# Cross attention, eight batches on one core: the maximum of half 1 is taken off by accumulating DMAs, and three left sums are made later

## The chip, the cores and the metric

The kernel runs on one core of one Trainium2 chip. A core has five engines with an instruction queue each: PE (TensorE, the matmuls, with its weight loads shown apart as PEld), DVE (VectorE), ACT (ScalarE), POOL (GpSimd) and SP (SyncE, which here only issues DMAs). Sixteen DMA engines move data for all queues. The time is device microseconds of one launch; the median of three runs of the kernel before is 704.6 us (703.48 to 705.7).

## The reference

For each of 8 batches there are two inputs of 512 channels by 1024 positions, `x1` and `x2`. Cut to what matters:

```python
q = einsum('bcn,dc->bnd', x1, Wq) + bq            # d = 64
k = einsum('bcn,dc->bdn', x2, Wk) + bk[:, None]
v = einsum('bcn,dc->bdn', x2, Wv) + bv[:, None]   # 512 channels
attn = softmax(einsum('bnd,bdm->bnm', q, k), axis=2)
out = einsum('bcm,bnm->bcn', v, attn) + x1
```

All of it is float32. The softmax runs over the 1024 keys m, for each of the 1024 queries n.

## The kernel before, in words

**The mathematics.** The scores are kept transposed, keys on the partitions and queries along the free axis. The kernel first makes y = x2 times exp(scores), divides its columns by the sums of the exponentials, and then makes Wv times y, adds the bias and x1. Both large products ("first" with `stage` y, "second" with `stage` o) are done with seven block products in place of eight (`MULT`): each factor is cut into two by two blocks, and DVE makes sums and differences of blocks (S1 to S4 on the left, T1 to T4 on the right). Three of the seven block products of the first product, numbers 2, 3 and 4, are cut once more in the same manner (`multiply_2`, `multiply_3`, `multiply_4`, with `inner_left` and `inner_right` for their sums and L351 for their matmuls).

**The tiles.** `e[h]` holds the exponentials of half h of the queries (h = 0 for queries 0 to 511, 1 for the rest): 128 partitions x 2 halves of the keys x 4 key tiles x 512 queries. Block 11 of the right factor is `e[0][:, 0]`, 21 is `e[0][:, 1]`, 12 is `e[1][:, 0]` and 22 is `e[1][:, 1]`. The blocks of x2, transposed, are `a["11"]` to `a["22"]`. S1 = 21 + 22, S2 = S1 - 11, S3 = 11 - 21 (written over block 21), S4 = 12 - S2. `u1`, `u5`, `u6`, `r` are tags of scratch tiles; a tag with one buffer makes the next user wait until the last reader of the tile is done.

**A period.** `period` handles one batch s. PE runs in this order: first(1), `multiply_2`, first(6), the scores of half 0 of the next batch n, the queries of the batch after it (L148, `ps_q`), first(5), first(7), `multiply_3`, the scores of half 1 of n, the keys of the batch after it (`ps_k`), `multiply_4`, and then the seven second products 1, 6, 2, 5, 7, 3, 4. In periods 1 to 7 this is all; in period 0 the products are not cut a second time. Period 6 has no queries and keys to project, and period 7 has no next batch.

**The softmax of the next batch** lies inside the period of this one. ACT copies the scores of a half from PSUM into `e[h]` (L197, L199). `fold` (L211) takes the maximum over the key tiles on DVE, `highest` folds the two key halves (L215) and lets POOL reduce over the partitions with one PARTITION_ALL_REDUCE into `top[h]` (L220), which has the same value on all partitions. `exponentials` then takes `top` off each key tile on DVE (L248, 128 x 1024 elements) and lets ACT raise it to the exponential (L249), four times for a half.

**The sums of the exponentials.** For half 0, `start_sum` copies the first key tile on ACT (L507) and adds the other three with accumulating DMAs that POOL issues, each waiting for the one before (L509). `total` folds the two key halves on DVE (L215), lets POOL reduce over the partitions (L225) and sends one row on by a small DMA (`few`, L227). For half 1 the sum is made on DVE (`sums`). `shares` makes the reciprocals (L233) and spreads them with two DMAs (L235, L237) over `den`.

**What sets the order.** The schedule is written by hand: each engine executes its instructions in the order of the source, and the framework puts in the waits. A wait stops all that stands behind it on that engine's queue. DMAs with accumulation are issued by POOL, plain ones by SP (and the copies of q by ACT).

**The places that the change touches**, in the order of the period:

- after first(5): the exponentials of half 0 of n (L248, L249), `start_sum`, `inner_right(s, 3, ...)`, and then the left sums S1, S2, S3 of n (L109), three DVE instructions of 128 x 1024 elements;
- after the scores of half 1: the folds of the maximum of half 1, `highest`, and for s.b > 0 `total(n, 0)`;
- `multiply_4`: its inner products are copied by ACT (L360) into `d` and `v`; `complete` (L422) adds v to d on DVE, two more additions (L432) bring it into `u6`. The tile `v` has the tag `u1`, which is also the tag of the tile that second(1) is copied into (L312);
- `evict_y(s, "21")` (L462, L464) makes the last block of y, which second(2) reads;
- the second products: ACT copies the banks of 1, 6 and 5 (L312) into u1, u6, u5 for later additions; the chain 1, 6, 5, 3 runs on one pair of PSUM banks, so product 6 may add to a bank only after ACT has copied product 1 out of it;
- the four exponentials of half 1 of n stand after second(6) and after second(5);
- `evict_o` adds bank, bias and an earlier copy on DVE (L496), or, for block 12, copies the bank with the bias on ACT (L492, into tag `r`); then POOL issues a DMA that adds x1 to it (L499), and SP writes it out (L500).

In period 0 the order differs a little: there S1, S2 and S3 of batch 1 and the inner sums of its `multiply_2` stand between the last blocks of the result, and `total(1, 0)` behind second(2).

Of the kernel before, what the change touches and what calls it, by code (L numbers as in the profile page):

```python
# [10 lines left out]
AF = mybir.ActivationFunctionType  # L11
ALU = mybir.AluOpType
# [3 lines left out]
def kernel(  # L16
# [46 lines left out]
    nc = tc.nc  # L63
    P = 128
# [3 lines left out]
    H = 512  # L68
    MH = N // P // 2
# [64 lines left out]
    def sum_a(s, *ks):  # L134
        for k in ks:
            if k != "S3":
                s.a[k] = sb.tile([P, MH, C // 2], F32, tag=f"a{k}", name=f"a{k}_{s.b}")
        left_sums(s.a, *ks)
# [74 lines left out]
    def fold_halves(s, h, op):  # L213
        f = s.mx[h]
        nc.vector.tensor_tensor(f[:, 0, :], f[:, 0, :], f[:, 1, :], op)  # L215
# [6 lines left out]
    def total(s, h):  # L222
        fold_halves(s, h, ALU.add)
        s.den[h] = sb.tile([P, H], F32, tag="den", name=f"den_{s.b}_{h}", bufs=2)
        nc.gpsimd.partition_all_reduce(s.den[h], s.mx[h][:, 0, :], P, ReduceOp.add)  # L225
        s.few[h] = sb.tile([P, H // P], F32, tag="few", name=f"few_{s.b}_{h}", bufs=2)
        nc.gpsimd.dma_start(  # L227
            s.few[h], s.den[h][0:1, :].rearrange("o (p f) -> o p f", p=P)
        )
# [9 lines left out]
    def first_exponentials(s, g, i):  # L239
# [2 lines left out]
        nc.vector.tensor_tensor(e, e, s.top[0], ALU.subtract)  # L242
        nc.scalar.activation(e, e, AF.Exp)  # L243

    def exponentials(s, h, i):
        e = s.e[h][:, :, i, :]
        top = s.top[h].unsqueeze(1).to_broadcast([P, 2, H])
        nc.vector.tensor_tensor(e, e, top, ALU.subtract)  # L248
        nc.scalar.activation(e, e, AF.Exp)  # L249
# [77 lines left out]
    def inner_left(s, i, x, tag):  # L327

        v = {f"{p + 1}{q + 1}": x[:, ts(q, MH // 2), ts(p, P)] for p in range(2) for q in range(2)}
        sums = sb.tile([P, 4, MH // 2, P], F32, tag=tag, name=f"aI{i}_{s.b}")  # L330
        for z, (k, x, y, op) in enumerate(LEFT):
            v[k] = sums[:, z]
            nc.vector.tensor_tensor(v[k], v[x], v[y], op)
        s.inner[i] = v

    def inner_right(s, i, x, tag):

        v = {
            f"{q + 1}{r + 1}": x[:, ts(q, MH // 2), ts(r, H // 2)] for q in range(2) for r in range(2)
        }  # L340
        sums = sb.tile([P, 4, MH // 2, H // 2], F32, tag=tag, name=f"eI{i}_{s.b}")
        for z, (k, x, y, op) in enumerate(RIGHT):
            v[k] = sums[:, z]
            nc.vector.tensor_tensor(v[k], v[x], v[y], op)
        s.inner[i, "t"] = v
# [18 lines left out]
    def inner_bank(s, i, z):  # L364
        return ps_s.tile([P, 2, H], F32, tag="sc", name=f"ps_i{i}{z}_{s.b}")[:, 0, left]
# [35 lines left out]
    def multiply_onto(s, i, d_tag, v_tag):  # L401

        b0, b1 = (s.bank[MULT[i][2], j] for j in range(2))
        chain, third = inner_bank(s, i, 0), inner_bank(s, i, 2)
        d = sb.tile([P, 2, 2, H // 2], F32, tag=d_tag, name=f"d{i}_{s.b}")
        v = sb.tile([P, 2, H], F32, tag=v_tag, name=f"v{i}_{s.b}")[:, 0, left]
        for z, ps, opens, *copies in (
            (1, chain, True, d[:, 0, 0, :]),  # L410
            (7, third, True, v),
            (6, chain, False, d[:, 1, 0, :]),
            (2, b0[:, left], False),
            (5, chain, False, d[:, 0, 1, :], d[:, 1, 1, :]),
            (4, b1[:, left], False),
            (3, b0[:, right], False),
        ):
            inner_product(s, i, z, ps, opens, *copies)

        def complete():  # L420
            both = v.unsqueeze(1).to_broadcast([P, 2, H // 2])
            nc.vector.tensor_tensor(d[:, 1], d[:, 1], both, ALU.add)  # L422

        return d.rearrange("p j a n -> p j (a n)"), complete

    def multiply_4(s):

        d, complete = multiply_onto(s, 4, "u5", "u1")
        complete()
        for j in range(2):  # L430
            u6 = s.tmp[6][:, j, :]
            nc.vector.tensor_tensor(u6, u6, d[:, j, :], ALU.add)  # L432
# [175 lines left out]
    def period(s, n, nn, nnn):  # L608

        def first(i):
            multiply(s, "y", i, s.a, s.t, MH)

        def second(i):
            multiply(s, "o", i, w, s.y, 2)

        open_t(s)
        if n is None:
            load_x(s, x1)  # L620
        first(1)
        if s.b == 0:
            head_second(s, n)
        sum_e(s, "T1", "T2")
        if s.b == 0:
            total(s, 0)
        else:
            shares(s, 0)
        if n:
            load_a(n, "11")  # L630
        if s.b == 0:
            first(2)
            evict_y(s, "11", (1,))
            keys(n)
            load_x(nn, x1)
            sum_t4(s)
            sums(s, 1)
            shares(s, 0)
        else:
            evict = multiply_2(s)  # L640
            if s.b > 1:
                sums(s, 1)
            evict()
            sum_t4(s)
            sum_a(s, "S4")
            if s.b == 1:
                sums(s, 1)
        sum_e(s, "T3")
        if n:
            load_a(n, "21", "22")  # L650
        first(6)
        if s.b:
            inner_right(s, 4, s.t["T4"], "eT2")
            inner_left(s, 3, s.a["S4"], "aI3")

        def next_queries():
            queries(nn)
            load_x(nn, x2)

        def next_keys():  # L660
            keys(nn)
            if nnn:
                load_x(nnn, x1)

        if n:
            scores_and(n, 0, "c", next_queries if nn else nothing)
            for i in range(1, MH):
                fold(n, 0, i, "max", ALU.max)
            highest(n, 0)
        shares(s, 1)  # L670
        first(5)
        if n:
            for i in range(MH):
                exponentials(n, 0, i)
            start_sum(n, 0)
        if s.b:
            inner_right(s, 3, s.t["22"], "eT1")
            if n:
                sum_a(n, "S1", "S2", "S3")
        first(7)  # L680
        if s.b > 1:
            inner_left(s, 4, s.a["22"], "a12")
        if s.b:
            evict_y(s, "22", (1,))
            multiply_3(s)()
            for k in ("11", "12", "22"):
                evict_y(s, k, (2,))
        else:
            evict_y(s, "11", (2,))
            evict_y(s, "22")  # L690
            first(3)
            evict_y(s, "12", (1,))
        if s.b == 1:
            inner_left(s, 4, s.a["22"], "a12")
        if n:
            scores_and(n, 1, "a", next_keys if nn else nothing)
        sum_y(s, "T1")
        sum_y(s, "T2")
        if n:
            if s.b == 0:  # L700
                left_sums(w, "S1", "S2", "S3", "S4")
            for i in range(1, MH):
                fold(n, 1, i, "max", ALU.max)
            highest(n, 1)
            if s.b:
                total(n, 0)
        if s.b:
            multiply_4(s)
        else:
            first(4)  # L710
        if n:
            load_a(n, "12")
        evict_y(s, "21")
        second(1)
        sum_y(s, "T3")
        sum_y(s, "T4")
        second(6)
        if n:
            exponentials(n, 1, 0)
            exponentials(n, 1, 1)  # L720
        second(2)
        evict_o(s, "11")
        if s.b == 0:
            total(n, 0)
        second(5)
        if n:
            exponentials(n, 1, 2)
            exponentials(n, 1, 3)
        second(7)
        evict_o(s, "22")  # L730
        if n:
            if s.b:
                inner_left(n, 2, n.a["12"], "aS4")
            else:
                sum_a(n, "S1")
            second(3)
            evict_o(s, "12")
            if s.b:
                inner_right(n, 2, n.e[0][:, 1], "eT4")
            else:  # L740
                sum_a(n, "S2")
            second(4)
            evict_o(s, "21")
            if s.b == 0:
                sum_a(n, "S3")
                inner_left(n, 2, n.a["12"], "aS4")
                inner_right(n, 2, n.e[0][:, 1], "eT4")
        else:
            second(4)
            evict_o(s, "21")  # L750
            second(3)
            evict_o(s, "12")
# [37 lines left out]
```

## Time and profile before

| | us |
|---|---|
| median of 3 runs | 704.6 (703.48 to 705.7) |
| the profiled execution, its own time | 704.53 |
| its span in the profile | 702.8 |
| PE busy | 689.1, 2144 matmuls |
| DVE busy | 601.5, 730 instructions |
| ACT busy | 251.4, 390 instructions |
| POOL busy | 173.6, 135 instructions |
| POOL-issued DMAs (queue q0) | 29.96 MB, 25.2% of 16 engines' span |
| SP-issued DMAs (queue q1) | 70.26 MB, 29.3% of 16 engines' span |

The span is what the profiler saw from the first to the last instruction; 1.7 us of the execution's own time lie outside it. PE ran at full clock throughout (0.999 of it granted). A busy PE means that matmuls follow one another; how far each could be shorter is not in this number. The chain of waits, which follows the work that ended last back to its start, lies on PE for 80% of the span and on DVE for 12%.

The groups that the change removes, moves or adds to:

| line and group | count | mean of one | what it is |
|---|---|---|---|
| L248 DVE subtract, 128 x 1024 | 60 | 1251 ns | maximum taken off; 28 of them are half 1 of batches 1 to 7 |
| L249 ACT exponential, 128 x 1024 | 60 | 1054 ns | |
| L109 DVE S1, S2, S3, 128 x 1024 | 8 each | 1219, 1315, 1218 ns | |
| L220 POOL reduction of the maximum | 16 | 2026 ns | |
| L225 POOL reduction of the sum | 16 | 3497 ns | |
| L509 POOL issue of an accumulating DMA | 21 | 1205 ns | |
| L312 ACT copy of a bank, 128 x 512 | 48 | 586 ns | second product |

### The profile page before, as it was taken

To read this page: it belongs to the slowest core of one execution; us is meant where nothing else is said; L and a number is where in the kernel's file an instruction comes from. 1 tells how busy PE (TensorE), PEld (TensorE's weight loads), DVE (VectorE), ACT (ScalarE), POOL (GpSimd) and SP (SyncE) were. 2 spreads that over 40 slices of the span, in tenths; PEclk is the share of its full clock that TensorE was granted. 3 is DMA by queue.
4 is the path that set the end of the run, shared out by engine and by line. 5 is a ranking of instruction groups with operands and counts; after the bars stand their busy time and mean duration, and the time that the engine had idled before them with its cause. 6 is when DMAs were issued, how large, how long until landed. Compare 5 with 4: busy or idle time off the path is not lost.

```text
span 702.8 us, 6246 instructions
## 1 busy us (share of the span) xinstructions
PE 689.1 (98%) x2144; PEld 346.3 (49%) x2144; DVE 601.5 (86%) x730; ACT 251.4 (36%) x390; POOL 173.6 (25%) x135
## 2 busy tenths in 40 slices
PE   8999999999999999999999999999999999899997
PEld 4333444535545455454654556454554545545563
DVE  0998776989989899798998989889898889989584
ACT  2733424146231543225432344423444136232120
POOL 0124314132423123221142222222231222322000
PEclk9999999999999999999999999999999999999999
DMA  9666375864558454765639467285643824269003
GB/s 331 222 214 233 92 209 94 185 196 81 181 103 232 145 101 155 156 187 150 129 118 185 153 173 187 60 181 159 156 89 63 207 76 76 60 107 268 15 1 120
DMA packets 41248, 102.72 MB, mean 146 GB/s; under 512 B 4608, under 2 KB 4608, under 8 KB 41216
## 3 DMA queue, kind: packets, MB, share of 16 engines
q1 hardware_dynamic: 24256, 70.26, 29.3%
q0 software_dynamic: 15696, 29.96, 25.2%
q10 hardware_dynamic: 1264, 2.10, 0.9%
q8 instruction: 17, 0.28, 0.2%
q14 instruction: 15, 0.12, 0.1%
HBM read 72.62 MB, written 16.81 MB: 127 GB/s over the span
## 4 chain that ended last, share of the span: by engine, by line
PE 80%; DVE 12%; DMA 4%; issue 2%; ACT 1%; SPq 1%; POOL 1%; DVEq 0%; ACTq 0%
PE ps_ya L301 21%; PE ps_oa L301 14%; PE ps_oc L301 12%; PE ps_i L351 11%; PE ps_yc L301 7%; PE ps_s L190 5%; PE ps_q L148 3%; PE ps_k L148 3%; PE ps_ya L351 3%; DVE max L211 2%; PE ps_yc L351 2%; DMA a<-in_x2T_dram 1%; DMA x_in_x_dram<-in_x_dram 1%; DVE y L464 1%; DVE e L248 1%
## 5 line engine op out<-in xcount | busy, mean ns | idle before, releaser
L301 PE MATMUL ps_ya<-eT,aS 128*128 128x512 f32 x256 | 113.1, 595 | 0.0
L312 ACT COPY uy<-ps_ya 128x512 f32<-128x512 f32 x48 | 28.1, 588 | 163.7 <-PE ps_ya L301 157.4
L248 DVE TENSOR_TENSOR e<-e,top 128x1024 f32<-128x1024 f32 x60 | 72.0, 1251 | 15.5 <-POOL top L220 15.5
L301 PEld LDWEIGHTS ps_ya<-eT,aS 128*128 128x128 f32 x256 | 48.0, 190 | 60.9 <-issue 59.4
L249 ACT ACTIVATE e<-e 128x1024 f32<-128x1024 f32 x60 | 61.5, 1054 | 27.9 <-DVE e L248 26.4
L220 POOL PARTITION_ALL_REDUCE top<-max x16 | 32.4, 2026 | 146.2 <-DVE max L215 75.3
L301 PE MATMUL ps_yc<-e,a 128*128 128x512 f32 x144 | 63.4, 593 | 0.0
L225 POOL PARTITION_ALL_REDUCE den<-sum x16 | 56.0, 3497 | 22.8 <-DVE sum L215 17.8
L351 PE MATMUL ps_i<-eI,aI 128*128 128x256 f32 x252 | 60.4, 380 | 1.2 <-ACT sum L507 1.1
L301 PE MATMUL ps_oc<-y,w 128*128 128x512 f32 x128 | 57.7, 593 | 1.3 <-DVE y L464 1.3
L301 PE MATMUL ps_oa<-yT,w_S 128*128 128x512 f32 x128 | 57.6, 593 | 1.2 <-ACT uo L312 1.2
L301 PE MATMUL ps_ya<-e,a 128*128 128x512 f32 x128 | 56.3, 593 | 0.8 <-ACT e L243 0.8
L199 ACT COPY e<-ps_s 128x1024 f32<-128x1024 f32 x47 | 46.7, 1027 | 22.3 <-PE ps_s L190 21.3
L312 ACT COPY uo<-ps_oa 128x512 f32<-128x512 f32 x48 | 27.8, 586 | 74.9 <-PE ps_oa L301 60.5
L496 DVE SCALAR_TENSOR_TENSOR uo<-ps_oc,bv_sb,uo 128x512 f32<-128x512 f32 x42 | 30.9, 747 | 27.3 <-PE ps_oc L301 25.1
L351 PEld LDWEIGHTS ps_i<-eI,aI 128*128 128x128 f32 x252 | 47.2, 190 | 9.1 <-ACT sum L507 1.8
L499 POOL DMA_DIRECT2D uo<-in_x_dram x21 | 25.0, 1189 | 104.0 <-DVE uo L496 98.0
L254 DVE TENSOR_TENSOR eT<-e,eT 128x1024 f32<-128x1024 f32 x32 | 48.8, 1545 | 0.5
L190 PE MATMUL ps_s<-q,k 64*128 64x512 f32 x188 | 47.3, 608 | 1.6 <-ACT q L524 0.8
L509 POOL DMA_DIRECT2D sum<-e x21 | 25.3, 1205 | 78.2 <-DMA sum<-e 58.7
L301 PEld LDWEIGHTS ps_yc<-e,a 128*128 128x128 f32 x144 | 27.3, 190 | 34.8 <-issue 33.6
L211 DVE TENSOR_TENSOR max<-max,e 128x1024 f32<-128x1024 f32 x32 | 39.2, 1225 | 3.7 <-ACT e L197 0.5
(117 smaller groups left out, 1063.7 us busy)
## 6 DMA issues: line engine op xcount, KB each, us to landing
x_in_x_dram<-in_x_dram SPq DMA_DIRECT2D x60, 512.0 KB, 6.0
a<-in_x2T_dram SPq DMA_DIRECT2D x32, 512.0 KB, 6.7
sum<-e POOLq DMA_DIRECT2D x21, 512.0 KB, 5.0
uo<-in_x_dram POOLq DMA_DIRECT2D x21, 512.0 KB, 5.9
out_dram<-uo SPq DMA_DIRECT2D x21, 512.0 KB, 4.5
x_head<-in_x_dram SPq DMA_DIRECT2D x8, 512.0 KB, 8.2
den<-row POOLq DMA_DIRECT2D x16, 256.0 KB, 3.6
r<-in_x_dram POOLq DMA_DIRECT2D x7, 512.0 KB, 6.0
```

The lines of the kernel that those rows point to most:

```text
L148: nc.tensor.matmul(ps[r, :], w_sb[:, c, :], s.x[:, c, ts(h, H)], start=(c == 0), stop=(c == CT - 1),)
L190: nc.tensor.matmul(ps[g], s.k[r, ts(i, P)], s.q[r, ts(h, H)], start=True, stop=True)
L199: nc.scalar.copy(e[:, :, i, :], whole)
L211: nc.vector.tensor_tensor(f, e[:, :, 0, :] if i == 1 else f, new, op)
L220: nc.gpsimd.partition_all_reduce(s.top[h], s.mx[h][:, 0, :], P, ReduceOp.max)
L225: nc.gpsimd.partition_all_reduce(s.den[h], s.mx[h][:, 0, :], P, ReduceOp.add)
L248: nc.vector.tensor_tensor(e, e, top, ALU.subtract)
L249: nc.scalar.activation(e, e, AF.Exp)
L254: nc.vector.tensor_tensor(t[k], t[x], t[y], ALU.subtract)
L301: nc.tensor.matmul(ps, left[ka][:, k, ts(j, P)], right[kb][:, k, :], start=opens and k == 0, stop=i in (2, 3, 4) and k == n_k - 1, skip_gr ...
L312: nc.scalar.copy(s.tmp[i][:, j, :], ps)
L351: nc.tensor.matmul(ps, s.inner[i][ka][:, k, :], s.inner[i, "t"][kb][:, k, :], start=opens and k == 0, stop=z in (2, 3, 4) and k == MH // 2 ...
```

## The change

The four DVE subtractions of half 1 are gone. In their place `lower` lets ACT multiply `top` by -1 in place, and POOL issue four DMAs that add this tile, repeated for the two key halves, to the four key tiles of `e[1]` (512 KB each). The four exponentials then stand together behind the ACT copies of second(5). `lower` and, behind it, `total(n, 0)` now follow `multiply_4`. S1, S2 and S3 of n move from behind first(5) to behind the first block of the result, for all batches alike. The tile `v` of `multiply_4` takes the tag `r`. Batch 0 keeps its subtractions on DVE.

```diff
+    def lower(s, h):
+        top = s.top[h]
+        nc.scalar.mul(top, top, -1.0)
+        for i in range(MH):
+            nc.gpsimd.dma_start(
+                s.e[h][:, :, i, :], top.unsqueeze(1).to_broadcast([P, 2, H]), accum_op=ALU.add
+            )
+
+    def lowered_exponentials(s, h):
+        for i in range(MH):
+            e = s.e[h][:, :, i, :]
+            nc.scalar.activation(e, e, AF.Exp)
...
     def multiply_4(s):
-        d, complete = multiply_onto(s, 4, "u5", "u1")
+        d, complete = multiply_onto(s, 4, "u5", "r")
...
             inner_right(s, 3, s.t["22"], "eT1")
-            if n:
-                sum_a(n, "S1", "S2", "S3")
         first(7)
...
             highest(n, 1)
-            if s.b:
-                total(n, 0)
         if s.b:
             multiply_4(s)
         else:
             first(4)
+        if n:
+            lower(n, 1)
+            if s.b:
+                total(n, 0)
         if n:
             load_a(n, "12")
         evict_y(s, "21")
...
         second(6)
-        if n:
-            exponentials(n, 1, 0)
-            exponentials(n, 1, 1)
         second(2)
         evict_o(s, "11")
         if s.b == 0:
             total(n, 0)
+        if n:
+            sum_a(n, "S1", "S2", "S3")
         second(5)
         if n:
-            exponentials(n, 1, 2)
-            exponentials(n, 1, 3)
+            lowered_exponentials(n, 1)
         second(7)
         evict_o(s, "22")
         if n:
-            if s.b:
-                inner_left(n, 2, n.a["12"], "aS4")
-            else:
-                sum_a(n, "S1")
+            inner_left(n, 2, n.a["12"], "aS4")
+            inner_right(n, 2, n.e[0][:, 1], "eT4")
             second(3)
             evict_o(s, "12")
-            if s.b:
-                inner_right(n, 2, n.e[0][:, 1], "eT4")
-            else:
-                sum_a(n, "S2")
             second(4)
             evict_o(s, "21")
-            if s.b == 0:
-                sum_a(n, "S3")
-                inner_left(n, 2, n.a["12"], "aS4")
-                inner_right(n, 2, n.e[0][:, 1], "eT4")
```

## The prediction

> **What bounds the kernel now.** I read the totals first, then the busy time by stage, with the cuts laid where PE begins a new period, and then the orders of the single engines in one period that runs smoothly and in one that doesn't.
>
> ```profile
> PE 689.1 (98%) x2144; PEld 346.3 (49%) x2144; DVE 601.5 (86%) x730; ACT 251.4 (36%) x390; POOL 173.6 (25%) x135
> ...
> 122.50:209.00 86.50, 85.11 (x270) 43.31 (x269) 80.82 (x102) 32.08 (x50) 23.21 (x17) 1.00 0.59 148
> 209.00:293.50 84.50, 84.50 (x270) 43.60 (x269) 75.94 (x93) 31.99 (x50) 22.23 (x17) 1.00 0.61 154
> 462.40:546.90 84.50, 84.50 (x270) 43.59 (x269) 75.65 (x93) 31.99 (x50) 22.24 (x17) 1.00 0.53 127
> 546.90:629.00 82.10, 78.49 (x237) 41.02 (x236) 75.85 (x93) 29.93 (x47) 22.24 (x17) 1.00 0.44 100
> ```
>
> A stage's row has its length, then the busy time of PE, PEld, DVE, ACT and POOL. Periods 2 to 5 are full: PE is busy for all of their 84.5 us, so taking work off DVE is worth nothing there. Gain can come only from period 1 (86.50 against 84.46 us, 2.0 lost) and period 6. Period 6 lacks two projections, each 3.59 us in a full period, so it should take 77.28 us; the chain of waits has its first matmul at 546.87 and that of period 7 at 629.05, 82.18 us, so 4.9 are lost. Period 0 and period 7 show no such waits apart from the head and the tail, which the change doesn't touch. The most that could be had is some 7 us, 1%.
>
> PE in period 6 (start, length, and in brackets the wait):
>
> ```profile
> 590.59 1.99 PE L190 MATMUL ps_s<-q,k 64*128 64x512 f32 x8
> 593.94 1.13 PE L190 MATMUL ps_sa<-q,k 64*128 64x512 f32 x4 [1.36 <-DVE y L442]
> ...
> 602.43 3.60 PE L301 MATMUL ps_oa<-y,w 128*128 128x512 f32 x8
> 607.18 3.70 PE L301 MATMUL ps_oa<-yT,w_S 128*128 128x512 f32 x8 [1.16 <-ACT uo L312]
> 611.65 3.67 PE L301 MATMUL ps_oc<-y,w 128*128 128x512 f32 x8 [0.77 <-DVE y L464]
> ```
>
> Against the starts of the same steps in period 2 the loss is 0.40 in `multiply_3`, 1.64 in the scores of half 1, 0.42 in `multiply_4` (which starts late behind those score copies), 1.32 in second(1) and 1.04 in second(6): 4.82. DVE sets nearly all of it:
>
> ```profile
> 585.61 1.22 DVE L109 TENSOR_TENSOR aS<-a,a 128x1024 f32<-128x1024 f32 x1
> ...
> 592.60 1.29 DVE L442 TENSOR_TENSOR y<-ps_ya,d 128x512 f32<-128x512 f32 x2
> ...
> 603.72 0.69 DVE L215 TENSOR_TENSOR max<-max 128x512 f32<-128x512 f32 x1
> 604.33 0.68 DVE L215 TENSOR_TENSOR sum<-sum 128x512 f32<-128x512 f32 x1
> 604.93 1.53 DVE L422 TENSOR_TENSOR d<-d,v 128x512 f32<-128x512 f32 x1
> 606.38 3.33 DVE L432 TENSOR_TENSOR uy<-uy,d 128x512 f32<-128x512 f32 x2
> ```
>
> The three sums S1 to S3 stand from 585.61 to 589.14 ahead of L442, for which the scores wait.
>
> **S1 to S3 moved.** DVE loses 3.5 us of work before L442. In period 6 what follows comes up to two limits: L422 needs the ACT copies, done at 589.6, and L442 the end of `multiply_3` on PE at 590.6. In period 2, where DVE waits there for ACT, L442 starts 0.14 us before the PE step behind it; so it starts at 590.45, 2.15 earlier than at 592.60. The scores then take 3.63 and `multiply_4` 6.15 us: 1.64 + 0.42 won, and second(1) starts at 600.37. The sums go to where the four subtractions were, 3.5 us in place of 4.7 per period, between two evictions that wait for PE (281.1 to 285.0 in period 2: 281.07 + 3.5 = 284.6). They cost nothing; that cover has 0.4 us to spare, and the eviction behind it another 4 before second(4) needs the bank.
>
> **The tag of `v`.** Second(1)'s copy (L312) no longer waits for L422, which in period 6 held ACT until 606.5. In its place stands the new multiplication by -1, ahead of L312 on ACT's queue, and it waits for POOL's reduction of the maximum.
>
> ```profile
> 267.69 2.15 POOL L220 PARTITION_ALL_REDUCE top<-max  x1 [7.05 <-DVE max L215]
> 269.74 3.59 POOL L225 PARTITION_ALL_REDUCE den<-sum  x1
> ...
> 281.45 1.20 POOL L499 DMA_DIRECT2D uo<-in_x_dram  x1 [7.21 <-DVE uo L496]
> ...
> 271.20 0.59 ACT L312 COPY uo<-ps_oa 128x512 f32<-128x512 f32 x1 [2.80 <-PE ps_oa L301]
> ...
> 283.70 2.00 ACT L249 ACTIVATE e<-e 128x1024 f32<-128x1024 f32 x2
> 288.37 0.69 ACT L492 ACTIVATE r<-ps_oa,bv_sb 128x512 f32<-128x512 f32 x1 [2.66 <-PE ps_oa L301]
> ```
>
> The multiplication isn't in the trace; ACT on 128 x 512 takes 0.59 (L312) to 0.69 us (L492), and it can't be below nothing. I take 0.6. In period 2 the reduction ends at 269.84, the multiplication at 270.5, and the copy at 271.20 isn't held; PE needs it only at 272.72. In period 6 the reduction ends at about 604.5 (2.15 us earlier than 606.66), the multiplication at 605.15, the first copy at 605.65, and second(6) starts at 605.75: 1.43 earlier than at 607.18, though 1.95 later than PE could. Behind it second(2) needs block 21 of y. DVE has it at 607.8: 602.2 for the fold, 1.2 for L422, 1.4 for L432, 0.6 for the fold of the sum, 2.4 for L462 and L464. Second(2) starts at 609.2 in place of 611.65: **2.45 won in period 6**, with 0.40 + 1.95 left.
>
> L432 takes 1.4 and not 3.33 because POOL's sum reduction, which lay beside it, now comes 4.8 us later, behind four DMA issues; two L432 without it take 1.29 (period 7). In period 2 it then lies beside the additions T3 and T4 of y, wanted by second(7) and second(4) some 4 and 11 us on. The Trainium skill (SBUF — State Buffer, "Who interferes with whom") says more than that: a DVE instruction with two SBUF inputs stands still for the whole of a POOL instruction that reads SBUF. By it L432 would have lost 3.59 us and not the 2.0 that the row shows; the sum would not change, since second(2) waits for PE in either case.
>
> **Period 1.** There DVE is late from 135.9 on, where the sums of half 1 stand behind `multiply_2`'s eviction, and that eviction waits for PE at 135.3. The 5 us that DVE gains at the end of period 0 are therefore lost again in waiting. The 1.12 us at `multiply_3` stay: PE waits there for ACT's exponentials of half 0. Behind the removed sums, L442 starts 0.6 earlier and L422 with block 21 follows at 189.3 in place of 192.0, before second(6) ends at 190.96. Of the 0.67 and 0.17 lost there 0.75 come back; the copy of second(1) ends at 187.2, just before PE wants it at 187.52.
>
> **The DMAs.** Each of 28 new DMAs is 512 KB from SBUF to SBUF, as L509's.
>
> ```profile
> sum<-e POOLq DMA_DIRECT2D x21, 512.0 KB, 5.0
> ...
> q0 software_dynamic: 272, 0.52, 54.7%
> ...
> 273.00:283.00 10.00, 10.00 (x24) 4.37 (x23) 10.00 (x12) 4.38 (x6) 2.13 (x3) 1.00 0.02 2
> ```
>
> The second line is one such DMA in the stretch 259.4 to 265.0: 54.7% of 5.6 us are 3.06 us of packets, which overlap a little; the slices show 190 to 205 GB/s for 2.8 us. It begins 1.9 us after its issue. The lowest price is thus 2.8 us each when they run one behind the other, the highest 6.0, the median from issue to landing of a DMA that adds x1 from HBM. I take 2.8, the same kind and size. POOL issues at 270.5, 271.7, 272.9, 274.1 and is free at 275.3; the sum reduction takes it to 278.9, and the eviction's DMA at 281.45 isn't delayed. The DMAs run from 272.4 to 283.6, through a stretch in which the last line shows the DMA engines busy for 2%. The last lands at some 284.2. ACT starts the exponentials at 283.8 behind the copies of second(5) and ends them by 287.9, before L492 at 288.37. T1 of the next period reads them at 294.2. `few`, now behind them in the queue, is wanted at 299. Cost nothing, with the limits below. SP's queue keeps its order, and its writes of the result wait, as before, for the evictions' DMAs. In period 0 the third sum DMA and the loads of x1 overlap; the last exponential ends there at about 117, T1 wants it at 123.2.
>
> The Trainium skill (DMA: Bandwidth & Descriptors, "Anatomy of one DMA — SWDGE (gpsimd) path") gives 2.0 us plus bytes over 436 GB/s. An estimate from that page is 3.2 us for one and 6.8 for four in a row. The trace has 5.0 for one. By the page's price the cover would be 7 us wider and the sum the same.
>
> **Sum.** 2.45 + 0.75 = 3.2 us. 704.53 - 3.2 = 701.3 for an execution like the profiled one; this one lay 0.07 below the median of the runs, so 701.4.
>
> **The rivals.** (1) *The DMAs land late*, slower. L492 must be done when first(1) of the next period takes its bank at 293.3, so the fourth DMA may land at 290.8; from 272.4 that is 4.6 us each. At 6.0 us each from 270.5 on the last lands at 294.5, the last exponential ends at 295.6, the first L492 at 296.3, 3.0 us late, in seven batches: 21 lost, 3 won, 722. For it: a source read twice is not in the trace, and these are four at once where L509's go singly. Against: same size, same packets, empty queues. (2) *POOL's reduction holds ACT*, no change. If the reduction takes 4.1 us as the longest of L225 does, and not 2.15, the copy in period 6 comes 1.95 later, at 607.6, and second(2) starts at 611.1: 0.5 won there. In period 1 the copy ends at 189.1, second(2) starts at 192.5 and not at 191.62: 0.9 lost; in each of periods 2 to 5 the copy ends at 273.0 and not before 272.72: 1.2 lost together. In all 1.6 lost, 706.2. For it: it overlaps DVE work as L225 does. Against: it does so already, at 2.15. (3) *DVE's lead carries through period 1*, so that all of its 2.0 us come back: 3.2 + 1.3, 700.1. For it: the 5 us are real. Against: the wait at 135.3. That the change doesn't do what it says can be left out: the built order of each engine has the 28 DMAs, and 28 subtractions fewer.
>
> **How the numbers follow.** The forecast has 0.56, its own range is 700.8 to 702.6 (the multiplication and the reduction each off by half a microsecond at both places). Rival 1 has 0.15, rival 2 0.19, rival 3 0.10. What the measurement can tell from no change is 0.3%, 2.1 us, that is below 702.5. Faster: 0.53 of the forecast and rival 3, 0.63. Same: the rest of the forecast and most of rival 2, 0.20. Slower: rival 1 and a little of rival 2, 0.17. The range 699.9 to 706.4 leaves out rival 1 and the edges of the others.
>
> **What would show it.** Periods 2 to 5 still 84.5 us with PE full; period 6 at some 79.7 and period 1 at 85.7; no wait on DVE L442; second(6) of period 6 waiting for L312 behind POOL's reduction; the last exponential of half 1 done 5 us before T1. A wait of first(1) for ACT in every period, or a first exponential that waits for its DMA beyond 284, makes the prediction wrong.

## The result and the profile after

The changed kernel takes 711.58 us (median of 4 runs, 710.95 to 716.0) where the kernel before, on the same chip, takes 704.34 (4 runs): a ratio of 1.0114, with a 95% interval of 1.007 to 1.0159. It is slower, and outside the range that was forecast. The profiled execution took 710.98 us, its span is 709.2 against 702.8. All ratios, here and below, are over fast runs alone, which leaves out a single run, that of 713.47 us in e2; they are not the quotients of the medians beside them.

Lines have moved by 14: L446, L478, L326, L374, L268, L510 and L514 are now what L432, L464, L312, L360, L254, L496 and L500 were; L248 is the multiplication by -1, L250 issues the new DMAs, L257 is the exponential behind them. L225 is in its place.

From the page of the changed kernel: the totals, and the landing times of four kinds of DMA (median us from issue to landing).

```profile
PE 689.8 (97%) x2144; PEld 345.7 (49%) x2144; DVE 584.0 (82%) x702; ACT 254.4 (36%) x397; POOL 204.3 (29%) x163
...
e<-top POOLq DMA_DIRECT2D x28, 512.0 KB, 9.4
sum<-e POOLq DMA_DIRECT2D x21, 512.0 KB, 5.0
uo<-in_x_dram POOLq DMA_DIRECT2D x21, 512.0 KB, 6.8
out_dram<-uo SPq DMA_DIRECT2D x21, 512.0 KB, 5.3
```

DVE has lost 28 instructions, but only 17.5 us of its 601.5: 28 subtractions at 1.25 us were 35. Something has become longer on DVE. PE's work is the same and its share is lower, so the time went into waits of PE. The writes of the result land in 5.3 us where they took 4.5, and the DMAs that add x1 in 6.8 where they took 5.9.

The busy time by stage, cut where PE begins periods 1, 2, 5 and 6 (columns as before):

```profile
122.30:207.90 85.60, 84.71 (x270) 43.48 (x269) 73.78 (x89) 32.50 (x51) 27.74 (x21) 1.00 0.74 173
207.90:295.30 87.40, 84.91 (x270) 43.30 (x269) 73.61 (x89) 32.38 (x51) 26.48 (x21) 1.00 0.76 177
...
467.50:554.10 86.60, 84.72 (x270) 43.49 (x269) 74.21 (x89) 32.39 (x51) 26.41 (x21) 1.00 0.68 149
554.10:633.70 79.60, 78.05 (x237) 41.26 (x236) 73.63 (x89) 30.36 (x48) 26.82 (x21) 1.00 0.61 125
```

Periods 1 and 6 are as forecast: 85.59 and 79.61 us by the starts of their first matmuls, against 86.50 and 82.19 before. The loss lies in the periods that were full. Periods 2 to 5 take 87.48, 86.59, 85.66 and 86.59 us in place of 84.46 each, and period 7 some 1.6 more. What PE waited for (us in total, times, longest):

```profile
PE ps_oc L315 <- DVE y L478: 6.2, 4, 1.9
PE ps_i L365 <- ACT i L374: 2.4, 2, 1.4
PE ps_oa L315 <- ACT uo L326: 1.2, 1, 1.2
```

The third wait was forecast; the first two are new. The timeline of period 2 shows the first (start, length, and in brackets the wait before it):

```profile
269.37 1.28 DVE L446 TENSOR_TENSOR uy<-uy,d 128x512 f32<-128x512 f32 x2
...
272.37 6.42 DVE L478 TENSOR_TENSOR y<-y,den 128x512 f32<-128x512 f32 x2
...
271.11 4.91 POOL L250 DMA_DIRECT2D e<-top  x4 [1.46 <-ACT top L248]
274.05 5.18 POOL L225 PARTITION_ALL_REDUCE den<-sum  x1
...
276.33 1.02 PE L315 MATMUL ps_oc<-y,w 128*128 128x512 f32 x2
278.84 2.84 PE L315 MATMUL ps_oc<-y,w 128*128 128x512 f32 x6 [1.49 <-DVE y L478]
```

The same step in period 2 of the kernel before:

```profile
274.01 1.28 DVE L464 TENSOR_TENSOR y<-y,den 128x512 f32<-128x512 f32 x2
...
276.15 3.60 PE L301 MATMUL ps_oc<-y,w 128*128 128x512 f32 x8
```

L478 makes block 21 of y, the last thing that second(2) needs, by two instructions of 128 x 512. The first takes 0.68 us. The second begins at 272.97 and takes 5.82, to 278.79; it ends just ahead of POOL's sum reduction (279.23). At 0.68 us it would have been over at 273.65, before the reduction's row begins. PE has begun second(2), and stands still until block 21 is there. In period 4 it is again the second that is held (5.26 us), in periods 3 and 5 it is the first (5.85 and 5.86), and PE loses a little more there than in period 2. In periods 1 and 6 both go through and the addition T3 behind them is held (5.79 and 5.83 us); PE doesn't wait for it.

The second wait is ACT's copy `i` of an inner product in `multiply_2` of the next period. The tile `i` has the tag u5, as has the tile from which block 22 of the result is written. ACT in period 2, the timeline:

```profile
217.10 0.37 ACT L374 COPY i<-ps_i 128x256 f32<-128x256 f32 x1 [1.67 <-DMA out_dram<-uo]
```

and the chain of waits at the start of period 7 (start, length, what):

```profile
633.91 0.47 DVE uo L510
634.38 8.98 DMA out_dram<-uo
643.35 0.02 issue
643.38 0.04 ACTq L374
643.41 0.04 issue
643.45 0.38 ACT i L374
```

A write of block 22 takes 8.9 and 9.0 us in the two places; the median of all writes of the result is 5.3. In period 2 of before it was issued at 210.19, took 4.9 and was done at 215.1, 1.7 ahead of the copy at 216.79. In the changed kernel it is issued at 208.14 and done at 217.0. PE begins period 2 there at 207.77 in place of 208.86, so the copy could have come 1.1 us earlier than before, at 215.7.

### The profile page after: what moved, and what is told of

The parts are those of the page before. It is cut to its first block, busy times and chain, and to the rows that moved or that the text cites. A ratio compares the mean times of both kernels' runs of the same rounds, so it can differ in the third digit from the quotient of the medians.

```text
span 709.2 us, 6289 instructions
## 1 busy us (share of the span) xinstructions
PE 689.8 (97%) x2144; PEld 345.7 (49%) x2144; DVE 584.0 (82%) x702; ACT 254.4 (36%) x397; POOL 204.3 (29%) x163
## 5 line engine op out<-in xcount | busy, mean ns | idle before, releaser
L326 ACT COPY uy<-ps_ya 128x512 f32<-128x512 f32 x48 | 28.1, 588 | 163.7 <-PE ps_ya L315 158.5
L220 POOL PARTITION_ALL_REDUCE top<-max x16 | 30.9, 1934 | 145.6 <-DVE few L233 73.6
L225 POOL PARTITION_ALL_REDUCE den<-sum x16 | 64.9, 4054 | 24.0 <-DVE sum L215 19.0
L326 ACT COPY uo<-ps_oa 128x512 f32<-128x512 f32 x48 | 28.0, 585 | 88.8 <-PE ps_oa L315 88.8
L478 DVE TENSOR_TENSOR y<-y,den 128x512 f32<-128x512 f32 x62 | 58.7, 1008 | 0.0
L510 DVE SCALAR_TENSOR_TENSOR uo<-ps_oc,bv_sb,uo 128x512 f32<-128x512 f32 x42 | 31.0, 747 | 21.9 <-PE ps_oc L315 12.9
L262 DVE TENSOR_TENSOR e<-e,top 128x1024 f32<-128x1024 f32 x32 | 37.0, 1220 | 14.4 <-POOL top L220 14.4
L268 DVE TENSOR_TENSOR eT<-e,eT 128x1024 f32<-128x1024 f32 x32 | 44.0, 1394 | 0.5
L315 PEld LDWEIGHTS ps_oc<-y,w 128*128 128x128 f32 x128 | 24.0, 190 | 38.2 <-issue 31.7
```

Source lines behind the costliest of these rows:

```text
L220: nc.gpsimd.partition_all_reduce(s.top[h], s.mx[h][:, 0, :], P, ReduceOp.max)
L268: nc.vector.tensor_tensor(t[k], t[x], t[y], ALU.subtract)
L315: nc.tensor.matmul(ps, left[ka][:, k, ts(j, P)], right[kb][:, k, :], start=opens and k == 0, stop=i in (2, 3, 4) and k == n_k - 1, skip_gr ...
L326: nc.scalar.copy(s.tmp[i][:, j, :], ps)
L478: nc.vector.tensor_tensor(y[:, j, :], y[:, j, :], rden, ALU.mult)
L510: nc.vector.scalar_tensor_tensor(o[:, j, :], s.bank[bank, j], bias(j), o[:, j, :], ALU.add, ALU.add)
```

## The experiments

All are edits of the changed kernel unless something else is said. Theory A lays the loss on the sum reduction's new place, theory B on the buffer that the copy `i` shares with a write that the new DMAs make late; rival B of e1 and e2 is another thing, the DMAs as a load. What a letter means in full stands in each expectation. Ratios are to the kernel before, run beside each; the experiments ran on three chips (e1 to e4, e5 to e8, e9 to e12), so across these groups a difference of medians is good to some 0.7 us, by which the kernel before differs among them.

| run | median us | from, to | ratio, 95% interval |
|---|---|---|---|
| e1, reduction ahead of `multiply_4` again | 735.26 | 733.54, 735.69 | 1.0422 (1.0392 to 1.0452) |
| e2, reduction behind the first block of the result | 704.32 | 700.67, 713.47 | 0.9993 (0.9967 to 1.0019) |
| e3, the 28 DMAs left out | 700.96 | 700.29, 701.31 | 0.9940 (0.9918 to 0.9962) |
| e4, subtractions on DVE, moves kept | 701.72 | 700.28, 702.78 | 0.9949 (0.9934 to 0.9964) |
| e5, own buffer for `i` | 707.87 | 707.64, 708.52 | 1.0039 (1.0024 to 1.0054) |
| e6, e2 and e5 together | 701.15 | 700.34, 701.54 | 0.9940 (0.9925 to 0.9955) |
| e7, before with the tag of `v` alone | 706.10 | 703.54, 707.11 | 1.0009 (0.9995 to 1.0023) |
| e8, e4 with the reduction ahead of `multiply_4` | 705.47 | 701.77, 707.45 | 1.0002 (0.9984 to 1.0019) |
| e9, e5 with the reduction one step later | 701.07 | 700.67, 701.29 | 0.9954 (0.9941 to 0.9966) |
| e10, e4 with the own buffer | 700.58 | 700.31, 700.79 | 0.9947 (0.9935 to 0.9960) |
| e11, e8 with the own buffer | 701.84 | 700.96, 702.23 | 0.9962 (0.9949 to 0.9974) |
| e12, before with the own buffer alone | 704.25 | 703.31, 704.68 | 0.9997 (0.9987 to 1.0006) |

**e1: the reduction back in its old place.**

```diff
             highest(n, 1)
+            if s.b:
+                total(n, 0)
...
             lower(n, 1)
-            if s.b:
-                total(n, 0)
```

> The changed kernel with total(n, 0) back in its old place, ahead of multiply_4, so that POOL reduces the sum before it issues the four DMAs; all else is as changed. Theory A (in the changed kernel POOL's reduction of the sum, dispatched behind the four DMA issues, keeps DVE's multiplication L478 of block 21 standing for 5.8 us, and second(2) waits for it, 7.3 us in periods 2 to 5): L478 takes 0.68 us each again, L446 is slowed to some 2.7 as before, periods 2 to 5 lose nothing at second(2); the DMAs run 3.6 us later, which can cost more at the waits for the results' writes, so 703 to 706.5 us. Rival B (the four DMAs themselves, as load on POOL and the DMA engines, cost the time): no better than the changed kernel, 710 us or more, since the DMAs come even later.

735.26 us: the worst of all, far above what theory A expected. By its number alone the run would speak for rival B; e6 and e9 below, at 701 us with all 28 DMAs in place, exclude that. The two L478 take 1.28 us together again, so it was what stands beside them in the new place that held them. But the reduction (3.59 us) now stands ahead of the multiplication and of the four issues, and the DMAs come later by so much. ACT of period 2 and 3 in e1:

```profile
297.85 1.06 ACT L257 ACTIVATE e<-e 128x1024 f32<-128x1024 f32 x1 [3.09 <-DMA e<-top]
...
305.41 0.59 ACT L326 COPY uy<-ps_ya 128x512 f32<-128x512 f32 x1 [5.34 <-DMA out_dram<-uo]
...
312.91 0.37 ACT L374 COPY i<-ps_i 128x256 f32<-128x256 f32 x1 [4.59 <-DMA out_dram<-uo]
```

The last exponential waits for its DMA, block 12 behind it comes late, and the writes of the result are late for two of their tiles. That the DMAs land late is the condition of the prediction's rival 1. The price is not the one that it named: PE never waits for L506 in this run, but six times for the copy `i`, 20.8 us in all.

**e2: the reduction behind the first block of the result**, where period 0 has it.

```diff
             lower(n, 1)
-            if s.b:
-                total(n, 0)
...
         evict_o(s, "11")
-        if s.b == 0:
+        if n:
             total(n, 0)
```

> The changed kernel with total(n, 0) behind evict_o of block 11 in all periods, as in period 0, so that POOL's reduction of the sum comes away from the four DMA issues, on S1 to S3. Theory A: no L478 above 0.7 us although the four DMA issues stand where they did, no wait of PE on L478, the reduction holds S1 to S3 for 2 to 4 us in place of it; 701 to 705 us. Theory A' (the back-to-back DMA issues themselves hold DVE's instructions with two SBUF inputs): one L478 of 3 us or so until the fourth issue is over at about 5 us behind the first, and PE waits little. Rival B: still 709 or more.

704.32 us, but scattered. In the profiled run (703.43) periods 3 to 5 are 84.46 us again. Its timeline of period 2:

```profile
272.21 1.28 DVE L478 TENSOR_TENSOR y<-y,den 128x512 f32<-128x512 f32 x2
...
282.99 3.15 DVE L109 TENSOR_TENSOR aS<-aS,a 128x1024 f32<-128x1024 f32 x1
...
271.54 4.91 POOL L250 DMA_DIRECT2D e<-top  x4 [1.46 <-ACT top L248]
282.29 3.76 POOL L225 PARTITION_ALL_REDUCE den<-sum  x1
```

The issues lie beside L478 as before and hold neither it nor T3 and T4 behind it; the reduction now holds S2 (the L109 of 3.15 us), which has time. What is left is the copy `i`, with 1.7 us of waits in this run.

**e3: without the 28 DMAs** (the maximum is not taken off the scores of half 1 of batches 1 to 7).

```diff
         nc.scalar.mul(top, top, -1.0)
-        for i in range(MH):
-            nc.gpsimd.dma_start(
-                s.e[h][:, :, i, :], top.unsqueeze(1).to_broadcast([P, 2, H]), accum_op=ALU.add
-            )
```

> The changed kernel without its 28 DMAs: the maximum is not taken off the scores of half 1 of batches 1 to 7. Theory A: POOL's reduction of the sum comes about 3 us after its DVE fold and lasts 3.2 to 3.6, one L478 takes up to 3 us, but block 21 is still in time in periods 2 to 5 (276.3 in period 2); no wait on the writes of the results in periods 2 and 7. Span 699 (702.8 of before less 3.75 won in periods 0, 1 and 6), so 700.8 us. If the waits of ACT on the writes of results in periods 2 and 7 stay (1.2 and 1.6 us), these are not the DMAs' doing but come from PE being earlier there, and it is 703 us.

700.96 us, every period from 2 to 5 at 84.46, no wait of `i` though PE is just as early. The whole loss hangs on the DMAs. It doesn't say by which way.

**e4: the moves and the tag, with the subtractions of half 1 on DVE.**

```diff
-            lower(n, 1)
...
         second(6)
+        if n:
+            exponentials(n, 1, 0)
+            exponentials(n, 1, 1)
...
-            lowered_exponentials(n, 1)
+            exponentials(n, 1, 2)
+            exponentials(n, 1, 3)
```

> Only the moves: S1 to S3 and total(n, 0) in their new places and the tag r, but the maximum of half 1 taken off by DVE as before, in the old places. Theory A: DVE has 8.2 us of work behind second(6) in place of 4.7, which fits between the evictions; the gains of periods 1 and 6 (0.9 and 2.6) stay, PE is full in periods 2 to 5; 701 us, faster than before. Rival C (the moves themselves lose, DVE is late at the end of each period): periods 2 to 5 above 85 us, 706 or more.

701.72 us: the moves alone beat both kernels. The reduction stands where the changed kernel has it, right ahead of the two L478, but with no DMA issues in front of it; it takes 3.23 us and the two L478 2.36 in place of 1.28.

**e5: an own buffer for `i`.**

```diff
-        uv = sb.tile([P, 4, H // 2], F32, tag="u5", name=f"i26_{s.b}")
+        uv = sb.tile([P, 4, H // 2], F32, tag="i26", name=f"i26_{s.b}")
```

> The changed kernel with a buffer of its own for the tile that ACT's copy i (L374, multiply_2) writes, in place of the one that it shares with the copy of second(5), which block 22 of the result is written from. Theory B: in periods 2 and 7 this copy waits for the write of block 22 only because the buffer is shared, and the write is late because the four new DMAs push it. Then the 1.2 us of period 2 and the 1.6 us at the start of period 7 go, second(2) still loses its 7.3 us in periods 2 to 5: 708.0 to 709.0 us. Rival: the late writes show up at the next tile of the result (u6, u1, or uo of second(5) itself), and nothing is won: 711 to 712 us.

707.87 us; its profile is 3.3 us shorter than that of the changed kernel, and the medians differ by 3.7. The waits for `i` are gone, the four for L478 still make 6.2. Periods 2 to 5 lose 1.76, 2.11, 1.21 and 2.11 us, 7.2 together: that is theory A's part.

**e6: both edits, e2 and e5.**

> The changed kernel with both: the sum reduction behind the first block of the result in all periods, and the own buffer for the copy i; all 28 DMAs stay. If the reduction's place (theory A) and the shared buffer (theory B) are the whole loss, all periods from 2 to 5 are 84.5 us, period 7 begins its products without a wait, and the time is 700.7 to 702.0 us, no longer scattered over more than 2 us. Rival: the DMAs cost by a further way (the writes of the result, the exponentials, T1), then it stays at 703.5 or more, or scattered.

701.15 us within 1.2 us, all four periods at 84.46. With all 28 DMAs in place nothing of the loss is left, though the write of block 22 in period 2 still takes 7.5 us. So no third way of the DMAs shows: the ratio is that of e3, which has none of them.

**e7: the kernel before, with the tag of `v` alone.** The edit is the one in `multiply_4`.

> The kernel before with the tag of v alone changed to r. The prediction's reasoning: in period 6 second(6) no longer waits 1.16 us for ACT L326 behind DVE L422, but second(2) waits for block 21 of y from DVE all the same, so nothing is won: 704.2 to 704.8 us. Rival: the tag brings the 1.2 us of its own, 703.4 us.

706.1 us, by the interval no different from before, and not faster. In period 6 the wait of second(6) is gone and comes back, longer, at second(2), which waits for block 21 of y from DVE as was said. Its profile shows a price that wasn't foreseen; PE in period 6 of e7:

```profile
606.46 3.60 PE L301 MATMUL ps_oa<-yT,w_S 128*128 128x512 f32 x8
612.25 5.37 PE L301 MATMUL ps_oc<-y,w 128*128 128x512 f32 x8 [2.19 <-DVE y L464]
```

The eight matmuls behind the wait take 5.37 us in place of 3.67. The last section has more on this.

**e8: e4 with the reduction ahead of `multiply_4`.**

> The version with the moves of S1 to S3 and the tag r, the subtractions of half 1 on DVE, but the sum reduction of half 0 back ahead of multiply_4. By the prediction's term for the moved reduction, the additions L446 take 3.3 us again in place of 1.4, block 21 comes 1.9 us later in period 6 and second(2) waits for it, so 1.9 us of the gain are lost: 703.0 to 704.0 us, against 701.7 us with the reduction behind multiply_4. Rival: the reduction's place is worth nothing once the sums are moved, 701.4 to 702.0 us.

705.47 us, but scattered over 5.7 us, with three waits for `i` in its profile; it doesn't settle the question. e11 repeats it without these waits. Set beside e11 it says something else: the two kernels differ by the buffer of `i` alone and neither has the 28 DMAs, yet e8 is 3.6 us above e11 by the medians, 2.8 by the ratios.

**e9: e5, with the reduction one step later.**

```diff
             lower(n, 1)
-            if s.b:
-                total(n, 0)
...
         evict_y(s, "21")
+        if n and s.b:
+            total(n, 0)
```

> The changed kernel with the own buffer for the copy i and the sum reduction moved by one step only: behind the eviction of block 21 of y in place of ahead of it. All 28 DMAs stay. Theory A (the reduction, once handed to POOL behind the four DMA issues, holds DVE's next instruction with two SBUF inputs): the two L478 run in 1.3 us before the reduction is handed over, second(2) no longer waits in periods 2 to 5, and the hold falls on T3 or T4, wanted later: 700.7 to 702.0 us, 6 to 7 us below the version with the own buffer alone (707.9). Rival: four DMA issues ahead of the reduction hold DVE, or the reduction so late holds T3 for second(7): 704 us or more.

701.07 us, 6.8 below e5. Its timeline of period 2:

```profile
270.88 1.28 DVE L478 TENSOR_TENSOR y<-y,den 128x512 f32<-128x512 f32 x2
272.08 0.68 DVE L215 TENSOR_TENSOR sum<-sum 128x512 f32<-128x512 f32 x1
272.68 1.21 DVE L268 TENSOR_TENSOR y<-y,y 128x1024 f32<-128x1024 f32 x1
273.82 4.61 DVE L268 TENSOR_TENSOR yT<-y,yT 128x1024 f32<-128x1024 f32 x1
...
270.21 4.91 POOL L250 DMA_DIRECT2D e<-top  x4 [1.46 <-ACT top L248]
273.17 5.18 POOL L225 PARTITION_ALL_REDUCE den<-sum  x1
...
275.44 3.60 PE L315 MATMUL ps_oc<-y,w 128*128 128x512 f32 x8
```

POOL's rows are those of the changed kernel: the reduction begins 2.96 us after the first issue (2.94 there) and takes 5.18. Only DVE's order is another. Two L478 run in 1.28, the fold of the sum stands behind them, and the hold falls on T4, which is wanted by second(4) 10 us on. It does so in every period from 1 to 6 but the third, where T3 and T4 take 1.21 us each and nothing is held. This one step of the order is 6.8 us by the medians, 6.0 by the ratios and 6.5 by the profiles.

**e10, e11, e12: what the moves are worth, and the own buffer by itself.**

> The version with the moves alone (subtractions of half 1 on DVE, no new DMAs), with the own buffer for the copy i. If the scatter of that version (700.3 to 702.8) is this copy's wait, the time is 700.2 to 700.9 us, within 1 us from run to run; the 28 DMAs then bring nothing over it. Rival: the scatter is something else, 701.7 us as before.

> The same with the sum reduction back ahead of multiply_4 (the run of this version without the own buffer was scattered from 701.8 to 707.5 by the copy's wait). By the prediction's term block 21 is late in period 6 and second(2) waits 1.5 us as in that profile: 701.8 to 702.8 us, 1.5 us or so above the version with the reduction behind multiply_4. Rival: the place of the reduction is worth nothing, both alike.

> The kernel before with the own buffer alone. In its profile this copy never waits, so the time should be that of before, 704.0 to 704.7 us, and only its runs above 705.5 should go. Rival: before loses to this wait as well, 703 us.

e10 has the lowest median, 700.58 us, within half a microsecond. Against it the 28 DMAs, in the two versions where they cost nothing (e6 and e9), bring no gain that the runs can tell: the ratios are 0.9940 and 0.9954 beside 0.9947, with intervals that overlap. DVE's busy time is 591.9 us in e10 and 564.4 in e6, and periods 2 to 5 are at 84.46 us in both. e11 is at 701.84, so the reduction behind `multiply_4` is worth 1.3 us. e12 is the kernel before, 704.25 beside 704.22: the own buffer is worth nothing there. Whether this copy is behind the runs of before that lie higher on the other chips (up to 708.33) is open: on this chip there were none above 705.42.

## Why the prediction was wrong, point by point

**What failed first: the sum reduction's new neighbour.** The prediction said of it: "In period 2 it then lies beside the additions T3 and T4 of y, wanted by second(7) and second(4) some 4 and 11 us on", and took nothing for it. It put POOL free at 275.3 and the reduction behind that. Its own row is not far off that (274.05, and the fourth issue ends at 276.0). But in periods 2 to 5 DVE is held from an L478 on that starts 0.7 to 1.2 us ahead of the reduction's row (at 272.97 in period 2, where POOL is at its third issue). T3 would have started 0.6 us later. Measured, this is 7.2 us in periods 2 to 5 (e5), and e9 shows that the forecast would have held with the reduction one step later: there the hold is on T4, and costs nothing, as said. In periods 1 and 6 the hold lies on T3 in the changed kernel too, where the forecast had it, and the gain of these periods came.

The size failed as well. The only sizes that the prediction had were the reduction's own length, 3.59, and 2.0 by the row of L432. The hold is 5.82 against 0.68 for the same instruction unheld, 5.1 us, and it lasts until the reduction is nearly over, which itself comes behind four issues: from the end of the fourth to its own end are 3.2 us, its whole length in e4. With no issues in front (e4) the hold is 1.1 us, in e2, behind one issue, 1.9. What decides which instruction is the first to be held is not shown: the first L478 of period 2 starts 1.1 us after the fold that the reduction waits for, and is free.

The Trainium skill (SBUF — State Buffer, "Who interferes with whom") has the rule that would have warned: a DVE instruction with two SBUF inputs contends with a POOL instruction that reads SBUF, and the order of issue decides who stands still. The prediction cited it beside L432, from where the reduction was taken away, and didn't ask it again for the place where it was put. These runs agree with the rule on who is held: L478 and T4 have two SBUF inputs, DMA issues alone hold neither (e2). What they add is the start: the hold can begin ahead of the reduction's row.

**What failed second: "the eviction's DMA at 281.45 isn't delayed", and the writes of the result "as before".** In period 2 the DMA that adds x1 to block 11 is issued right behind DVE (282.84) and lands 5.7 us later, as before. The price forecast for the 28 DMAs was right too: 2.8 us each made 272.4 to 283.6, and in the windows of the changed kernel the DMA engines are full over this stretch (length, engines, then the clock, the DMA share and GB/s):

```profile
272.50:284.00 11.50, 10.01 (x24) 4.25 (x23) 11.40 (x8) 2.27 (x4) 8.49 (x6) 1.00 1.08 182
```

But in periods 1 and 6, where PE is earlier, the DMA for block 11 lands 7.2 and 7.0 us after its issue, in place of 5.6 and 5.7. In period 1 the write of block 11 then lies beside that of block 22, which takes 8.9 us in place of 4.9, and 6.0 without the 28 DMAs (e3); in period 6 it takes 9.0 in place of 7.1. That the one delay makes the other is read from the rows and not tested. In the same edit PE became 0.9 us earlier in period 1 and 2.6 in period 6, so the next user of the tile came earlier. No line of the prediction asked who waits for these writes. The price was 3.3 us (e5 against the changed kernel, profile to profile). The shared buffer is needed for it: with the DMAs and a buffer of its own the late write (8.9 us in period 1 of e9 as well) costs nothing. The DMAs are not the only way to it: an equally early PE without them doesn't wait in e3, but it does in e8, which loses some 3 us against e11 by the shared buffer.

**What held.** S1 to S3 moved: the wait of the scores for DVE (L442 before) is gone. Period 6 takes 79.61 us (79.7 forecast, 2.58 won for 2.45), period 1 85.59 (85.7). PE in period 6 of the changed kernel:

```profile
613.00 3.70 PE L315 MATMUL ps_oa<-yT,w_S 128*128 128x512 f32 x8 [1.18 <-ACT uo L326]
616.54 3.60 PE L315 MATMUL ps_oc<-y,w 128*128 128x512 f32 x8
```

Second(6) waits for ACT's copy behind POOL's reduction of the maximum, and second(2) doesn't wait, both as worked out; the wait is shorter, 1.18 us where second(6) was put 1.95 later than PE could. The multiplication by -1 takes 0.63 us (0.6 taken). The exponentials follow the copies of second(5) without a wait and L506 is on time. The term for the reduction beside L432 was 1.9 us (3.33 to 1.4); e11 less e10 gives 1.3: with it gone second(2) still waits 0.58 us in e10 for L478, which the reduction now holds in its new place. For e9 and e6, the same change without the two losses, 701.4 us would have been right to 0.4.

**The rivals.** None of them was what happened. Rival 1 (DMAs late) is not in the changed kernel, whose exponentials are on time; in e1, where the DMAs start a reduction later, they are late, and PE waits at another place than that rival said. Rival 2 (a longer reduction of the maximum) did not come: it takes 1.78 us in period 2 and 2.15 in period 6, where that rival had 4.1. Rival 3 fell: period 1 is 85.59 and not 84.46. Two rivals that lose time were missing: the reduction holding L478 in periods 2 to 5, and the copy `i` waiting for a write of the result.

## What to carry to other kernels

When an instruction that holds another engine is moved, go through what stands beside its new place from the moment its input is ready, not from where its row is expected to begin; a queue of DMA issues ahead of it makes the hold longer. Moving it one step in the other engine's order can be worth everything (here 6 to 7 us), and taking work off an engine that isn't the bound is worth nothing (e10 against e6). Where an edit makes the bounding engine earlier or a queue fuller, look for tiles that share a buffer with a pending write, and give them one of their own first.

## What the runs showed of the hardware

**A long wait of PE can cost more than itself.** Behind waits of 1.88 us and less, the clock granted in the next 8 us was 1.00 in the profiles of before, of the changed kernel, e1, e2, e7 and e8. Behind the wait of 2.19 us in e7 it fell to 0.50 one microsecond later and stayed there for 3.41 us; behind those of 2.62, 3.27, 3.91, 4.28 and 5.17 us in e1 it was 0.50 for 3.4 to 6 us. No wait between 1.88 and 2.19 us was seen, so these runs don't place the boundary, nor show that the length of the wait alone decides. The windows of e1 behind one of 3.91 us:

```profile
313.34:318.40 5.06, 5.06 (x12) 4.07 (x13) 0.83 (x2) 0.75 (x2) 4.15 (x3) 0.50 1.10 247
```

This accounts for what e1 lost beyond its 20.8 us of waits for `i`, at least in the main: PE is busy for 702.1 us there and for 687.6 in e6, with the same 2144 matmuls. It also accounts for the period 6 of e7, 83.94 us against 82.19: its second(2) takes 1.7 us longer. The Trainium skill (TensorE: Matmul & The Clock Gate, "What's actually happening") puts the half clock after at least one idle window of about 3.4 us; here a wait of 2.19 us was enough.

**An issue of a DMA doesn't hold DVE, what is queued behind it does.** In period 2 of the changed kernel the first L478 runs beside the second and third issue in 0.68 us. In period 2 of e2 the two L478 run beside the first three in 1.28 us, and T3 and T4 beside the later ones in 1.21 each. With the reduction behind the same issues, one such instruction takes 5.3 to 5.9 us in each of periods 1 to 6 of the changed kernel.
